# One reciprocal for two row tiles of a softmax, and a list order made anew

## The chip, the cores and the metric

The kernel runs on one core of one Trainium2 chip. The core has a matrix engine (TensorE, PE in the profile), a vector engine (VectorE, DVE), an activation engine (ScalarE, ACT), a general engine (GpSimd, POOL) and a queue that issues most transfers (SyncE, SP). Each engine takes its instructions strictly in the order of the program, and an instruction that waits for another engine holds up all that stand behind it. The metric is the device time of one execution in microseconds (us), the median of several runs.

## The reference

The input is a matrix `x` of 384 rows (nodes of a graph) and 1024 columns, and a list of 6528 edges with a type each. The reference computes a layer norm and a ReLU, three projections, three more projections of their results, a masked softmax attention with 16 heads of width 64, and an output projection with a residual:

```
h = relu(layernorm(x))
q = h @ wq.T + bq;  k = h @ wk.T + bk;  v = h @ wv.T + bv
q2 = heads(q @ wiq.T + biq);  k2 = heads(k @ wik.T + bik);  v2 = heads(v @ wiv.T + biv)
scores = q2 @ k2.T / 8 + mask          # 16 heads, 384 x 384; mask is -inf where there is no edge
attn = softmax(scores)
out = x + concat(attn @ v2) @ wo.T + bo
```

## The kernel before

**Chunks and planes.** Each of the seven weight matrices is cut into eight chunks of 128x1024 (tile `raw`), loaded by SP. The 56 chunks have numbers: 0 to 7 are `wv`, 8 to 15 `wq`, 16 to 23 `wiv`, 24 to 31 `wk`, 32 to 47 are `wiq` and `wik` in turn, 48 to 55 are `wo`. A chunk is split into a high and a low plane (tile `whl`), so that three matmuls of lower precision make up one of high precision: `split_hi` on ACT (L124, L128 in the profile) rounds the chunk, `split_lo` on DVE (L135, L137) takes the rest. The third of a step's three matmuls (L450, L451, L452) needs the low plane. A chunk is eight such steps. `raw` has four buffers, so the load of chunk c waits until the low plane of chunk c-4 is made.

**Sums.** Forty more transfers (tile `scan`, L144) bring weight chunks in once more, and ACT sums their squares or absolute values (L149), for the bounds by which the planes are scaled. They share three buffers.

**The mask.** DVE compares each edge's key with the others, 51 instructions at L295 that are called detections here, to find duplicates; POOL then scatters the edge values to tables in memory (`tab`, L306), which SP had cleared before (L223), and reads them back. The tiles `rows` (L283) hold the keys; they come in three groups of three transfers, for detections 0 to 17, 18 to 35 and 36 to 50. POOL's additions for the mask's diagonal (`mask_base`, L288 and L290) stand among the scatters.

**Attention.** A score tile j = 3p + t is row tile t (128 rows) of head pair p, 24 in all, with two heads o = 0, 1. For each the chain is: `do_S` on PE (L711) into two PSUM banks; `do_ttr` on DVE (L719) adds the mask, writes the tile `e` and the row minimum; `do_exp` on ACT (L723) with the row sum; `recip` and `rscale` on DVE (L726, L730) for both heads of the tile at once; then the normalised values in two planes (tile `pp`): `do_hi` on ACT (L738, L740) and `do_lo` on DVE (L746), or, for a head that a table gives to POOL, `do_norm` on POOL (L733), `do_hi` on ACT and `do_lo` on POOL (L744); then a transposing transfer by SP, and `do_av` on PE (L760). There are four PSUM banks `s` for the scores, so tile j can start when DVE has read tile j-2; six tiles `e`, so the reading of tile j needs the low planes of tile j-3; and three banks `g` for the chunks. `qk_lo` (L702) takes a chunk of `wiq` or `wik` out of its bank; `ao_hi` and `ao_lo` (L764, L767) take the attention's output out. The output projection (`omm`, steps o(a, k) for seven column blocks a and eight chunks k) fills PE between the last score tiles and after them; `finish` (L788) adds the residual and the results leave by transfers of SP and ACT.

**Who sets the order.** The functions above are tasks in a table, each with an engine, an assumed duration and its dependencies. A list scheduler at the end of the kernel repeatedly takes the task that can start first by these assumed times, and among equals the one that is due first. The table `P` at the top holds the numbers that steer it: where score tiles and `do_av` stand in PE's list (`pre`, `rate`, `ds`, `da`), which heads go to POOL (`pool`), the order of the last output steps (`last`), corrections of due times (`due`) and allowances for latency (`slack`, `wait`, `late`, `gate`). On the chip only the order counts; the assumed times are gone.

Of the kernel before, what the change touches and what calls it, by code (L numbers as in the profile page):

```python
# [8 lines left out]
F32 = mybir.dt.float32  # L9
# [15 lines left out]

P = dict(
    pre=11.98,
    rate=2.66,
    avlag=7,
    slack=0.6,  # L30
    act0=6.72,
    dve0=4.77,
    pool0=8.64,
    pb=6,
    lead=3,
    first=[7],
    gate=3.2,
    mll=3.72,
    ds=[0.0, 0.0, 0.0, 0.0, 0.0, 0.0, 0.0, 0.47, 0.47, 0.47, 0.47, 1.09, 0.47, 1.58, 0.47, 0.47, 0.47, 1.04, 0.62,
        0.47, 0.23, 0.47, 0.47, 1.14],  # L40
    da=[1.19, 0.16, 1.23, 1.19, 1.19, -0.39, -0.39, -0.39],
    pool=[0, 1, 0, 1, 0, 1, 0, 1, 0, 1, 0, 1, 0, 1, 0, 1, 0, 1, 0, 1, 0, 1, 0, 1, 0, 0, 0, 1, 0, 1, 0, 1, 0, 1, 0,
        1, 0, 0, 0, 1, 0, 1, 0, 0, 0, 0, 0, 1],
    last=[5, 1, 2, 0, 3, 6, 4],
    sp=dict(row=5.6, bv=41.0, biv=55.0, turn=75.6, kb=88.0, v2t=111.14, gq=118.19, gk=126.86, ob=149.12),
    due=dict(v2l=-0.13, ss=0.11, gkd=-2.65, lo=1.37),
    wait=0.08,
    late=0.27,
    selat=3.85,
    selby=1.62,  # L50
)


# [1 line left out]
def gnn_kernel(ctx: ExitStack, tc: tile.TileContext, x, edges, erows, etw, wq, wk, wv, wiq, wik, wiv, wo,  # L55
# [648 lines left out]
    def do_S(j):  # L704
# [3 lines left out]
        for i, (a, b) in enumerate(((0, 0), (0, 1), (1, 0))):  # L708
            for o in range(2):
                r = slice(o * 64, o * 64 + 64)  # L710
                nc.tensor.matmul(sps[j][o][:, :N], q[r, a, t * 128:(t + 1) * 128], k[r, b, :],  # L711
                                 start=(i == 0), stop=(i == 2))

    def do_ttr(j, o):
        if o == 0:
            sts[j] = work.tile([128, 6], F32, tag="st", name="st", bufs=6)
            es[j] = {}
        es[j][o] = work.tile([128, N], F32, tag="e", name="e", bufs=EB)
        DVE.tensor_tensor_reduce(es[j][o], sps[j][o][:, :N], ma[:, j % 3, :], nscale, 3.0e38, OP.add, OP.min,  # L719
                                 sts[j][:, o:o + 1])  # L720

    def do_exp(j, o):
        ACT.activation(es[j][o], es[j][o], AF.Exp, bias=sts[j][:, o:o + 1], scale=-1.0, accum_out=sts[j][:, 2 + o:3 + o])  # L723

    def recip(j):
        DVE.reciprocal(sts[j][:, 4:6], sts[j][:, 2:4])  # L726

    def rscale(j):

        DVE.tensor_scalar(sts[j][:, 4:6], sts[j][:, 4:6], PSC, None, op0=OP.mult)  # L730

    def do_norm(j, o):
        POOL.tensor_tensor(es[j][o], es[j][o], sts[j][:, 4 + o:5 + o].to_broadcast([128, N]), OP.mult)  # L733

    def do_hi(j, o):
        pls[j, o] = work.tile([128, 2, N], F16, tag="pp", name="pp", bufs=PB)
        if (j, o) in ON_POOL:
            ACT.activation(pls[j, o][:, 0, :], es[j][o], AF.Copy)  # L738
        else:
            ACT.activation(pls[j, o][:, 0, :], es[j][o], AF.Copy, scale=sts[j][:, 4 + o:5 + o])  # L740

    def do_lo(j, o):
        if (j, o) in ON_POOL:
            POOL.tensor_tensor(pls[j, o][:, 1, :], es[j][o], pls[j, o][:, 0, :], OP.subtract)  # L744
        else:
            DVE.scalar_tensor_tensor(pls[j, o][:, 1, :], es[j][o], sts[j][:, 4 + o:5 + o], pls[j, o][:, 0, :],  # L746
                                     op0=OP.mult, op1=OP.subtract)

    def do_turn(j, o):
# [199 lines left out]
    for p in range(8):  # L949
        for n in ("iq", "ik"):  # L950
            c = W0 + 2 * p + (n == "ik")
            chunk_tasks(c)
            for k in range(KT):
                tasks["mm", c, k][3].append(("Qlo" if n == "iq" else "kl", k))
            task(("qhi", c), "ACT", 0.5, lambda c=c: qk_hi(c), [("mm", c, 7)], 0.2, n[1] + "2", [("S", 3 * p + 2)])
            task(("qlo", c), "DVE", 0.53, lambda c=c: qk_lo(c), [("qhi", c)])
        for j in range(3 * p, 3 * p + 3):
            t = j % 3
            task(("S", j), "PE", 0.56, lambda j=j: do_S(j),
                 [("qlo", W0 + 2 * p), ("qlo", W0 + 2 * p + 1), ("S", j - 1)], 0.2, "s s", [("ttr", j, 0), ("ttr", j, 1)])  # L960
            for o in range(2):
                task(("ttr", j, o), "DVE", 0.54, lambda j=j, o=o: do_ttr(j, o),
                     [("S", j), ("ms", j % 3), ("ttr", j, 0) if o else ("ttr", j - 1, 1), ("kf", 7)], 0.2, "e", [("lo", j, o)])
            for o in range(2):
                task(("exp", j, o), "ACT", 0.6, lambda j=j, o=o: do_exp(j, o), [("ttr", j, o)])
            task(("rec", j), "DVE", 0.11, lambda j=j: recip(j), [("exp", j, 0), ("exp", j, 1)])
            task(("rsc", j), "DVE", 0.2, lambda j=j: rscale(j), [("rec", j)])
            for o in range(2):
                pool = (j, o) in ON_POOL
                if pool:  # L970
                    task(("nrm", j, o), "POOL", 0.83, lambda j=j, o=o: do_norm(j, o), [("rsc", j)])
                task(("ehi", j, o), "ACT", 0.41, lambda j=j, o=o: do_hi(j, o),
                     [("nrm", j, o) if pool else ("rsc", j)], 0.2, "pp", [("turn", j, o)])
                task(("lo", j, o), "POOL" if pool else "DVE", 0.87 if pool else 0.55, lambda j=j, o=o: do_lo(j, o), [("ehi", j, o)])
                task(("turn", j, o), "SP", 1.25, lambda j=j, o=o: do_turn(j, o), [("lo", j, o), ("av", p - 2), "pt"], 1.6)
        task(("av", p), "PE", 1.66, lambda p=p: do_av(p),
             [("turn", j, o) for j in range(3 * p, 3 * p + 3) for o in range(2)] + [("av", p - 1)] + [("v2l", i) for i in range(6)],
             0.2, "a", [("aolo", p)])
        task(("aohi", p), "ACT", 0.56, lambda p=p: ao_hi(p), [("av", p), "home"])
        task(("aolo", p), "DVE", 0.53, lambda p=p: ao_lo(p), [("aohi", p)])  # L980
    for i in range(6):
        task(("res", i), "POOL", 1.2, lambda i=i: residual(i), [("xb", i // 2), "bob", ("lo", 23, 1)])
    OFROM = [[("S", J - 1)], [("o", 0, 0)], [("mm", 47, 0)], [("o", 2, 0)], [("o", 1, 0)], [("o", 4, 0)], [("o", 3, 0)]]
# [158 lines left out]
```

## Time and profile before

| what | us |
|---|---|
| median of 3 runs (lowest, highest) | 274.82 (272.44, 275.53) |
| the profiled execution | 274.47 |
| its span, first to last instruction | 272.8 |
| around the span | 1.67 |
| busy in the span: PE, DVE, ACT, POOL | 264.7, 215.4, 207.4, 134.7 |

The profile has a page with shares, slices and groups of instructions, and the trace behind it answers for single stretches. A row of the timeline gives start, duration, engine, line, operation, tiles and shape, and in brackets how long the engine was idle before it and what ended the wait. A matmul's record is longer than the step to the next one, since matmuls are pipelined; the pace is the distance of two starts.

### The profile page before, as it was taken

Reading aid. Unit: us, or ns where it says so; the run is one execution under the profiler, and the core shown is the slowest. Engines: PE = TensorE matmul, PEld = TensorE weight load, DVE = VectorE, ACT = ScalarE, POOL = GpSimd, SP = SyncE. Lnnn points to the kernel's source line nnn. Section 1 sums busy time; section 2 is a strip of 40 time slices with the busy share of each in tenths; the row PEclk is TensorE's granted clock in tenths of the full one; section 3 lists DMA queues with packets and bytes.
Section 4 is the critical chain, followed back from the end, with each engine's and each line's share of the span. In section 5 each row is a group of like instructions: output and inputs, shape, how many; then the busy total and the mean of one; then the engine's idle time right before and its main releaser. Section 6 shows DMA issues by size and latency. Waiting matters only on the chain. (4 is left out here: it accounts for less than half of the span.)

```text
span 272.8 us, 5010 instructions
## 1 busy us (share of the span) xinstructions
PE 264.7 (97%) x1636; PEld 188.3 (69%) x1636; DVE 215.4 (79%) x537; ACT 207.4 (76%) x394; POOL 134.7 (49%) x142
## 2 busy tenths in 40 slices
PE   7899999999999999999999999999999999999994
PEld 6899999999984444899996555555555554444552
DVE  3775578999995675658697999999899899989033
ACT  3886769879897997586978859998989898794100
POOL 5764685545475655466610005556771464335900
PEclk9999999999999999999999999999999999999999
DMA  6899998896999998989899974799999979956415
GB/s 236 267 307 416 369 406 321 221 412 248 353 340 367 382 407 285 320 286 322 268 345 404 356 274 154 118 198 203 231 202 160 248 153 171 324 114 117 87 46 187
DMA packets 58922, 72.44 MB, mean 266 GB/s; under 512 B 42640, under 2 KB 43280, under 8 KB 58896
## 3 DMA queue, kind: packets, MB, share of 16 engines
q1 hardware_dynamic: 56688, 70.26, 83.9%
q0 software_dynamic: 2064, 1.80, 2.3%
q8 instruction: 13, 0.21, 0.3%
q14 instruction: 13, 0.11, 0.1%
q10 hardware_dynamic: 144, 0.07, 0.1%
HBM read 59.27 MB, written 3.39 MB: 230 GB/s over the span
## 5 line engine op out<-in xcount | busy, mean ns | idle before, releaser
L452 PE MATMUL g<-g,whl 128*128 128x384 f32 (+1 forms) x304 | 100.7, 331 | 0.8 <-DVE whl L135 0.5
L450 PE MATMUL g<-g,whl 128*128 128x384 f32 (+1 forms) x304 | 101.3, 333 | 0.0
L451 PE MATMUL g<-g,whl 128*128 128x384 f32 (+1 forms) x304 | 100.6, 331 | 0.0
L306 POOL DMA_INDIRECT tab<-edge x51 | 58.9, 1154 | 40.6 <-DMA tab<-edge 27.2
L149 ACT ACTIVATE scan<-scan 128x1024 f32<-128x1024 f32 x40 | 42.1, 1052 | 16.0 <-DMA scan<-in_wik_dram 5.4
L733 POOL TENSOR_TENSOR e<-e,st 128x384 f32<-128x384 f32 x20 | 22.9, 1146 | 52.7 <-DVE st L726 28.4
L137 DVE TENSOR_TENSOR whl<-raw,whl 128x1024 fp32r<-128x1024 f32 x22 | 27.1, 1230 | 19.2 <-ACT whl L128 12.7
L452 PEld LDWEIGHTS g<-g,whl 128*128 128x128 f32 x176 | 33.0, 188 | 0.6 <-issue 0.6
L450 PEld LDWEIGHTS g<-g,whl 128*128 128x128 f32 x176 | 33.1, 188 | 0.3
L451 PEld LDWEIGHTS g<-g,whl 128*128 128x128 f32 x176 | 33.1, 188 | 0.0
L723 ACT ACTIVATE e<-e,st 128x384 f32<-128x384 f32 x48 | 28.9, 603 | 3.0 <-DVE st L719 3.0
L744 POOL TENSOR_TENSOR pp<-e,pp 128x384 f16<-128x384 f32 x20 | 22.1, 1110 | 15.2 <-ACT pp L738 15.1
L719 DVE CUSTOM_DVE_ANT_0 e<-s,ma,cols 128x384 f32<-128x384 f32 x48 | 27.3, 607 | 0.0
L128 ACT ACTIVATE whl<-raw 128x1024 fp32r<-128x1024 f32 x23 | 24.1, 1048 | 4.1 <-POOL edge L253 2.0
L135 DVE SCALAR_TENSOR_TENSOR whl<-raw,small,whl 128x1024 f16<-128x1024 f32 x16 | 21.0, 1321 | 4.7 <-ACT whl L124 4.7
L450 PE MATMUL s<-whl,g 128*128 128x512 f16 (+2 forms) x65 | 23.6, 363 | 0.5 <-DVE st L719 0.5
L451 PE MATMUL s<-whl,g 128*128 128x512 f16 (+2 forms) x65 | 23.6, 363 | 0.0
L452 PE MATMUL s<-whl,g 128*128 128x512 f16 (+2 forms) x65 | 23.5, 363 | 0.0
L124 ACT ACTIVATE whl<-raw,small 128x1024 f16<-128x1024 f32 x16 | 18.1, 1141 | 5.6 <-DMA raw<-in_wo_dram 4.4
L450 PEld LDWEIGHTS <-whl 128*128 128x128 f16 x128 | 12.5, 98 | 12.1 <-issue 4.9
L135 DVE SCALAR_TENSOR_TENSOR whl<-raw,cols,whl 128x1024 f16<-128x1024 f32 x16 | 20.6, 1294 | 0.0
L746 DVE SCALAR_TENSOR_TENSOR pp<-e,st,pp 128x384 f16<-128x384 f32 x28 | 20.0, 741 | 0.6 <-ACT pp L740 0.5
(184 smaller groups left out, 456.3 us busy)
## 6 DMA issues: line engine op xcount, KB each, us to landing
raw<-in_wv_dram SPq DMA_DIRECT2D x8, 512.0 KB
scan<-in_wiv_dram SPq DMA_DIRECT2D x8, 512.0 KB
raw<-in_wq_dram SPq DMA_DIRECT2D x8, 512.0 KB
scan<-in_wk_dram SPq DMA_DIRECT2D x8, 512.0 KB
raw<-in_wiv_dram SPq DMA_DIRECT2D x8, 512.0 KB
scan<-in_wiq_dram SPq DMA_DIRECT2D x8, 512.0 KB
raw<-in_wk_dram SPq DMA_DIRECT2D x8, 512.0 KB
scan<-in_wik_dram SPq DMA_DIRECT2D x8, 512.0 KB
```

Of the source, the lines that this page charges most:

```text
L128: nc.scalar.activation(hi, raw[w], AF.Copy)
L135: nc.vector.scalar_tensor_tensor(lo, raw[w], sc, hi, op0=OP.mult, op1=OP.subtract)
L137: (eng or nc.vector).tensor_tensor(lo, raw[w], hi.bitcast(F32), OP.subtract)
L149: ACT.activation(x, x, AF.Abs if n in ("iv", "o") else AF.Square, accum_out=l1[:, j, m:m + 1])
L306: nc.gpsimd.indirect_dma_start(out=tabs[c // RNG], out_offset=bass.IndirectOffsetOnAxis(ap=idx[:, c:c + 1], axis=0), in_=val[:, c:c + 1], ...
L450: nc.tensor.matmul(ps, lhi, rhi, start=first, stop=False)
L451: nc.tensor.matmul(ps, lhi, rlo, start=False, stop=False)
L452: nc.tensor.matmul(ps, llo, rhi, start=False, stop=last)
L719: DVE.tensor_tensor_reduce(es[j][o], sps[j][o][:, :N], ma[:, j % 3, :], nscale, 3.0e38, OP.add, OP.min, sts[j][:, o:o + 1])
L723: ACT.activation(es[j][o], es[j][o], AF.Exp, bias=sts[j][:, o:o + 1], scale=-1.0, accum_out=sts[j][:, 2 + o:3 + o])
L733: POOL.tensor_tensor(es[j][o], es[j][o], sts[j][:, 4 + o:5 + o].to_broadcast([128, N]), OP.mult)
L744: POOL.tensor_tensor(pls[j, o][:, 1, :], es[j][o], pls[j, o][:, 0, :], OP.subtract)
```

## The change

Two row tiles now share one tile of statistics (`st`, 12 columns instead of 6): row minima, sums and reciprocals of tiles j and j+1. `recip` and `rscale` run once for an even and an odd tile together, on 128x4 elements instead of twice on 128x2, after the four exponentials of both. So the even tile's normalisation waits for the odd tile's exponentials. There are 12 such pairs of instructions instead of 24.

The scheduler gets one more number, `dl`: it adds to the allowance after a transfer for the tasks that sum (`ss`), so that they stand later in ACT's list, behind tasks that need a weight load. All the steering numbers are new, and the order of every engine is made anew from them: score tiles follow each other more closely in PE's list (`rate`), and the table `pool` gives POOL 19 heads instead of 20.

```diff
-    rate=2.66,
+    rate=2.454,
...
-    late=0.27,
+    late=0.334,
+    dl=0.549,
...
+    def st(j, n, o):
+
+        c = 4 * n + 2 * (j % 2) + o
+        return sts[j // 2][:, c:c + 1]
+
     def do_ttr(j, o):
+        if o == 0 and j % 2 == 0:
+            sts[j // 2] = work.tile([128, 12], F32, tag="st", name="st", bufs=4)
         if o == 0:
-            sts[j] = work.tile([128, 6], F32, tag="st", name="st", bufs=6)
             es[j] = {}
...
     def recip(j):
-        DVE.reciprocal(sts[j][:, 4:6], sts[j][:, 2:4])
+        DVE.reciprocal(sts[j // 2][:, 8:12], sts[j // 2][:, 4:8])
 
     def rscale(j):
 
-        DVE.tensor_scalar(sts[j][:, 4:6], sts[j][:, 4:6], PSC, None, op0=OP.mult)
+        DVE.tensor_scalar(sts[j // 2][:, 8:12], sts[j // 2][:, 8:12], PSC, None, op0=OP.mult)
...
-            task(("rec", j), "DVE", 0.11, lambda j=j: recip(j), [("exp", j, 0), ("exp", j, 1)])
-            task(("rsc", j), "DVE", 0.2, lambda j=j: rscale(j), [("rec", j)])
+            if j % 2:
+                task(("rec", j), "DVE", 0.12, lambda j=j: recip(j), [("exp", i, o) for i in (j - 1, j) for o in range(2)])
+                task(("rsc", j), "DVE", 0.2, lambda j=j: rscale(j), [("rec", j)])
...
+    for j in range(0, J, 2):
+        for o in range(2):
+            tasks[("nrm" if (j, o) in ON_POOL else "ehi", j, o)][3].append(("rsc", j + 1))
...
-                start = max(start, end[d] + (0 if e[0] == eng else e[4] + (P["slack"] if eng == "PE" else P["late"] if e[0] == "SP" else P["wait"])))
+                start = max(start, end[d] + (0 if e[0] == eng else e[4] + (P["slack"] if eng == "PE" else P["late"] + (P["dl"] if n[0] == "ss" else 0.0) if e[0] == "SP" else P["wait"])))
```

Three places show what this does to the order. The line numbers of the changed kernel are one higher in its first part and seven higher from `do_ttr` on.

**DVE, detections and the low planes of chunks 6 and 7.** L295 is a detection, L137 the low plane of a chunk, L479 takes a `wv` chunk out of its bank, L301 and L302 make scatter indices. Before, from the low plane of chunk 6 (first row) to those of chunks 7 and 8 (last row but one, `x2`):

```order
L137 TENSOR_TENSOR whl<-raw,whl 128x1024
L295 SCALAR_TENSOR_TENSOR junk,edge<-rows,edge,upper 128x128
L301 SCALAR_TENSOR_TENSOR ed<-edge 128x3x2
L302 TENSOR_SCALAR edge<-ed,small 128x3x2
L295 SCALAR_TENSOR_TENSOR junk,edge<-rows,edge,upper 128x128 x4
L479 TENSOR_TENSOR f<-g,rrow 128x384 x2
L137 TENSOR_TENSOR whl<-raw,whl 128x1024 x2
L295 SCALAR_TENSOR_TENSOR junk,edge<-rows,edge,upper 128x128 x2
```

In the changed kernel the same place, from six detections ahead of the low plane of chunk 6 to the low plane of chunk 7 (L138, last row):

```order
L296 SCALAR_TENSOR_TENSOR junk,edge<-rows,edge,upper 128x128 x6
L138 TENSOR_TENSOR whl<-raw,whl 128x1024
L480 TENSOR_TENSOR f<-g,rrow 128x384
L302 SCALAR_TENSOR_TENSOR ed<-edge 128x3x2
L303 TENSOR_SCALAR edge<-ed,small 128x3x2
L296 SCALAR_TENSOR_TENSOR junk,edge<-rows,edge,upper 128x128 x9
L302 SCALAR_TENSOR_TENSOR ed<-edge 128x3x3
L303 TENSOR_SCALAR edge<-ed,small 128x3x3
L138 TENSOR_TENSOR whl<-raw,whl 128x1024
```

Ahead of the low plane of chunk 7, eleven detections and two index pairs that stood behind it now stand ahead, and one L479 went behind it. On SP the third clear of a table now stands ahead of the load of chunk 5 instead of behind it, one transfer of `rows` ahead of the load of chunk 6, and the last three transfers of `rows` around the loads of chunks 9 and 10, several transfers earlier than before. On POOL `mask_base` stands behind the sixth scatter instead of the third.

**DVE, the reciprocals of tiles 8 and 9.** Tile numbers stand in the names (`st_2287` is tile 8's, `st_2302` tile 9's). Before:

```order
L726 RECIPROCAL st_2287<-st_2287 128x2
L730 TENSOR_SCALAR st_2287<-st_2287 128x2
L702 SCALAR_TENSOR_TENSOR q2_2316<-g_2198,cols_277,q2_2316 128x384
L726 RECIPROCAL st_2302<-st_2302 128x2
L730 TENSOR_SCALAR st_2302<-st_2302 128x2
L767 SCALAR_TENSOR_TENSOR g1_1732<-a_2228,small_97,g1_1732 128x384
```

Changed, from the second head of tile 9 (L726 is now `do_ttr`, L136 a low plane of weights, L753 a low plane of the softmax):

```order
L726 ISA e_2319,st_2250<-s_2260,ma_105,cols_277 128x384
L726 ISA st_2250 128x1
L136 SCALAR_TENSOR_TENSOR whl_2059<-raw_2005,cols_277,whl_2059 128x1024
L753 SCALAR_TENSOR_TENSOR pp_2297<-e_2191,st_2158,pp_2297 128x384
L733 RECIPROCAL st_2250<-st_2250 128x4
L737 TENSOR_SCALAR st_2250<-st_2250 128x4
```

One pair of instructions on four columns has taken the place of two pairs.

**ACT, between the exponentials of tiles 5 and 6.** L723 (L730 after the change) is an exponential, L740 and L738 (L747 and L745) are high planes of the softmax, L124 (L125) is the high plane of a weight chunk, L696 (L697) that of a `q2` or `k2` tile. Before, from the last exponential of tile 5:

```order
L723 ACTIVATE e_2111,st_2083<-e_2111,st_2083 128x384
L740 ACTIVATE pp_2147<-e_2067,st_2066 128x384
L738 ACTIVATE pp_2150<-e_2076 128x384
L740 ACTIVATE pp_2172<-e_2084,st_2083 128x384
L723 ACTIVATE e_2168,st_2167<-e_2168,st_2167 128x384
L723 ACTIVATE e_2177,st_2167<-e_2177,st_2167 128x384
```

Changed:

```order
L730 ACTIVATE e_2119,st_2056<-e_2119,st_2056 128x384
L125 ACTIVATE whl_2146<-raw_2054,cols_277 128x1024
L125 ACTIVATE whl_2161<-raw_2097,cols_277 128x1024
L747 ACTIVATE pp_2174<-e_2057,st_2056 128x384
L745 ACTIVATE pp_2179<-e_2066 128x384
L730 ACTIVATE e_2159,st_2158<-e_2159,st_2158 128x384
L730 ACTIVATE e_2168,st_2158<-e_2168,st_2158 128x384
```

Two weight planes now stand between the exponentials of tile 5 and the high planes of tile 4.

On PE the number of matmuls is the same. The work that went behind a score tile is: for tile 10 five chunk steps, for tiles 8 and 11 four, for tile 20 one chunk step and eight output steps, for tile 23 six output steps. Seven score tiles that ran in pairs back to back now stand in two places (7 pairs and 10 single tiles instead of 11 and 2). The last `do_av` has three output steps more ahead of it, and the last output block is one of 256 columns instead of one of 512.

More of the change, by code (lines that the diff above doesn't have):

```diff
@@ L27 @@
     pre=11.98,
-    rate=2.66,
+    rate=2.454,
     avlag=7,
[L30 to L33, printed above, removed]
+    slack=0.619,
+    act0=6.919,
+    dve0=5.054,
+    pool0=8.306,
     pb=6,
@@ L36 @@
     first=[7],
[L37 to L42, printed above, removed]
+    gate=3.474,
+    mll=3.761,
+    ds=[0.0, -0.08, 0.0, 0.0, 0.0, 0.0, 0.0, 0.02, 0.47, 0.47, -0.35, 0.27, -0.35, 1.49, 0.38, 0.38, 0.38, -0.86,
+        0.53, 0.38, 0.14, 0.38, 0.37, 1.04],
+    da=[1.19, 0.16, 0.44, 0.69, -1.09, -1.16, -1.16, -1.72],
+    pool=[0, 1, 0, 1, 0, 1, 0, 1, 0, 1, 0, 1, 0, 1, 0, 1, 0, 1, 0, 1, 0, 1, 0, 1, 0, 0, 0, 1, 0, 0, 0, 1, 0, 0, 1,
         1, 0, 0, 0, 1, 0, 1, 0, 0, 0, 0, 0, 1],
-    last=[5, 1, 2, 0, 3, 6, 4],
-    sp=dict(row=5.6, bv=41.0, biv=55.0, turn=75.6, kb=88.0, v2t=111.14, gq=118.19, gk=126.86, ob=149.12),
-    due=dict(v2l=-0.13, ss=0.11, gkd=-2.65, lo=1.37),
+    last=[1, 0, 2, 6, 3, 4, 5],
+    sp=dict(row=5.6, bv=41.0, biv=55.55, turn=75.6, kb=88.0, v2t=111.14, gq=118.19, gk=126.86, ob=147.73),
+    due=dict(v2l=5.14, ss=0.11, gkd=-1.36, lo=1.37),
     wait=0.08,
-    late=0.27,
-    selat=3.85,
-    selby=1.62,
+    late=0.334,
+    dl=0.549,
+    selat=4.065,
+    selby=1.991,
 )
@@ L719, in do_ttr @@
         DVE.tensor_tensor_reduce(es[j][o], sps[j][o][:, :N], ma[:, j % 3, :], nscale, 3.0e38, OP.add, OP.min,
-                                 sts[j][:, o:o + 1])
+                                 st(j, 0, o))
     def do_exp(j, o):
-        ACT.activation(es[j][o], es[j][o], AF.Exp, bias=sts[j][:, o:o + 1], scale=-1.0, accum_out=sts[j][:, 2 + o:3 + o])
+        ACT.activation(es[j][o], es[j][o], AF.Exp, bias=st(j, 0, o), scale=-1.0, accum_out=st(j, 1, o))
     def recip(j):
-        DVE.reciprocal(sts[j][:, 4:6], sts[j][:, 2:4])
+        DVE.reciprocal(sts[j // 2][:, 8:12], sts[j // 2][:, 4:8])
     def rscale(j):
-        DVE.tensor_scalar(sts[j][:, 4:6], sts[j][:, 4:6], PSC, None, op0=OP.mult)
+        DVE.tensor_scalar(sts[j // 2][:, 8:12], sts[j // 2][:, 8:12], PSC, None, op0=OP.mult)
     def do_norm(j, o):
-        POOL.tensor_tensor(es[j][o], es[j][o], sts[j][:, 4 + o:5 + o].to_broadcast([128, N]), OP.mult)
+        POOL.tensor_tensor(es[j][o], es[j][o], st(j, 2, o).to_broadcast([128, N]), OP.mult)
     def do_hi(j, o):
@@ L739, in do_hi @@
         else:
-            ACT.activation(pls[j, o][:, 0, :], es[j][o], AF.Copy, scale=sts[j][:, 4 + o:5 + o])
+            ACT.activation(pls[j, o][:, 0, :], es[j][o], AF.Copy, scale=st(j, 2, o))
     def do_lo(j, o):
@@ L745, in do_lo @@
         else:
-            DVE.scalar_tensor_tensor(pls[j, o][:, 1, :], es[j][o], sts[j][:, 4 + o:5 + o], pls[j, o][:, 0, :],
+            DVE.scalar_tensor_tensor(pls[j, o][:, 1, :], es[j][o], st(j, 2, o), pls[j, o][:, 0, :],
                                      op0=OP.mult, op1=OP.subtract)
```

## The prediction

> **What bounds the kernel now.** I read the page first, its busy shares and its slices.
>
> ```profile
> span 272.8 us, 5010 instructions
> ...
> PE 264.7 (97%) x1636; PEld 188.3 (69%) x1636; DVE 215.4 (79%) x537; ACT 207.4 (76%) x394; POOL 134.7 (49%) x142
> ...
> PE   7899999999999999999999999999999999999994
> ...
> PEclk9999999999999999999999999999999999999999
> ```
>
> PE is busy in 97% of the span, in every slice but the first two and the last at 90% or more, at full clock. The number of matmuls stays. So time can only come from gaps in PE's row, and from what stands after its last matmul. The second view is stretches of the attention stage (columns: sum of the stretch, then busy time of PE, PE's weight loads, DVE, ACT, POOL, then granted clock, DMA share, GB/s).
>
> ```profile
> 160.00:200.00 40.00, 40.00 (x286) 21.98 (x285) 37.88 (x102) 38.14 (x86) 21.96 (x21) 1.00 0.85 182
> 226.00:247.00 21.00, 19.98 (x139) 9.96 (x136) 19.80 (x50) 17.67 (x41) 8.03 (x6) 1.00 0.90 201
> ```
>
> From 160 to 200 us PE never waits, though DVE and ACT are 95% busy behind it. From 226 to 247 PE loses 1.0 us and DVE is 94% busy. DVE's time is near the bound there and nowhere else counts. The third view is PE's timeline, searched for starts that are further apart than the step.
>
> ```profile
> 41.57 0.34 PE L451 MATMUL g<-g,whl 128*128 128x384 f32 x1
> 42.23 0.45 PE L452 MATMUL g<-g,whl 128*128 128x384 f32 x1 [0.32 <-issue]
> ...
> 148.97 0.33 PE L451 MATMUL g<-g,whl 128*128 128x384 f16 x1
> 149.80 0.34 PE L452 MATMUL g<-g,whl 128*128 128x384 f16 x1 [0.51 <-DVE whl L135]
> ...
> 232.58 0.38 PE L452 MATMUL g<-whl,g 128*128 128x512 f16 x1
> 233.51 0.27 PE L450 MATMUL g<-whl,g 128*128 128x256 f16 x1 [0.56 <-DVE k L702]
> ...
> 245.84 0.38 PE L452 MATMUL s<-whl,g 128*128 128x512 f16 x1
> 246.68 0.27 PE L450 MATMUL s<-whl,g 128*128 128x256 f16 x1 [0.46 <-DVE st L719]
> ```
>
> Four stalls carry nearly all. Start to start they are 0.66, 0.83, 0.93 and 0.84; less the usual step (0.17 for 384 columns, 0.21 to 0.22 for 512) they lose **0.49, 0.66, 0.72 and 0.62**, together 2.5 us. The first waits for the low plane of chunk 7, the second for that of chunk 33, the third for a bank that `qk_lo` of chunk 47 must empty, the fourth for the bank of the second head of tile 23. These four are all that a better order can win; the paired reciprocal can touch only the last two.
>
> **The change, part by part.** The sum is made against the profiled execution's 274.47 us, which is 0.35 below the median of 274.82, so the two stand for each other.
>
> *The reciprocals themselves.*
>
> ```profile
> 239.71 0.17 DVE L726 RECIPROCAL st<-st 128x2 f32<-128x2 f32 x1 [0.67 <-ACT e L723]
> 239.90 0.17 DVE L730 TENSOR_SCALAR st<-st 128x2 f32<-128x2 f32 x1
> 239.98 1.28 DVE L135 SCALAR_TENSOR_TENSOR whl<-raw,small,whl 128x1024 f16<-128x1024 f32 x1
> ...
> 15.13 0.17 DVE L342 RECIPROCAL lnt<-lnt 128x3 f32<-128x3 f32 x1
> ```
>
> From the reciprocal's start to the start of what follows the scaling is 0.27. No row has a reciprocal on four columns; three cost the same 0.17 as two, so four are taken at 0.17, and at most 0.34. Twelve pairs go: 12 x 0.27 = 3.2 us of DVE (1.2 if four columns cost twice). By the windows this hides behind PE except near the end.
>
> *(A) Chunk 7.*
>
> ```profile
> 32.12 0.34 DVE L295 SCALAR_TENSOR_TENSOR junk<-rows,edge,upper 128x128 bf16<-128x128 f32 x1
> 35.51 0.35 DVE L301 SCALAR_TENSOR_TENSOR ed<-edge 128x6 f32<-128x6 f32 x1
> 36.04 0.59 DVE L295 SCALAR_TENSOR_TENSOR junk<-rows,edge,upper 128x128 bf16<-128x128 f32 x1
> 36.57 0.60 DVE L295 SCALAR_TENSOR_TENSOR junk<-rows,edge,upper 128x128 bf16<-128x128 f32 x1
> 38.12 1.01 DVE L479 TENSOR_TENSOR f<-g,rrow 128x384 f32<-128x384 f32 x2
> 40.94 1.23 DVE L137 TENSOR_TENSOR whl<-raw,whl 128x1024 fp32r<-128x1024 f32 x1 [1.82 <-ACT f L483]
> ...
> 36.55 0.46 POOL L290 TENSOR_TENSOR ma<-ma,d 128x128 f32<-128x128 f32 x1
> ...
> 32.89 1.06 ACT L128 ACTIVATE whl<-raw 128x1024 fp32r<-128x1024 f32 x1
> ```
>
> Before, DVE idled 1.82 ahead of this low plane, which ended at 42.17. Now the high plane of chunk 6 (32.89) comes some 1.2 later, since a `rows` transfer goes ahead of its load: it ends at 35.15, its low plane at about 36.5. Then come one L479 (0.5), two index pairs (0.53 each, 35.51 to 36.04), nine detections and the low plane (1.23). A detection takes 0.34 alone and 0.60 beside POOL's `mask_base`: the pitch there is 0.53 (36.04 to 36.57), alone 0.26 less, 0.27. All alone the chain ends at 36.5 + 0.5 + 1.06 + 9 x 0.27 + 1.23 = 41.7; with five of them beside `mask_base`, which now stands three scatters later, at 43.1. Against 42.17 that is -0.49 (no stall at all is the floor) to +0.95. I take a middle, **+0.3**, because POOL's later place falls beside the last detections rather than the first.
>
> The same two rows bear on a rule. The Trainium skill, page "SBUF — State Buffer", section "Who interferes with whom", says that a VectorE instruction with two inputs in SBUF contends with a GpSimd instruction that reads SBUF, and that the second one blocks. By that rule all detections beside `mask_base` pay, and A would be +0.9 instead of +0.3, the sum 0.6 higher. The trace agrees as far as it goes (0.34 alone, 0.60 beside).
>
> *(B) Chunk 33.* The stall of 0.66 follows late weights; the sums (L149) now stand behind the weight planes in ACT's list, which should free ACT for them, but the loads themselves keep their slots on SP. If the sum had been the cause, all 0.66 goes; if a load comes one place later, 0.3 is added. I take **-0.1**, nearest to "nothing moved".
>
> *(C) The last two stalls.*
>
> ```profile
> L746 DVE SCALAR_TENSOR_TENSOR pp<-e,st,pp 128x384 f16<-128x384 f32 x28 | 20.0, 741 | 0.6 <-ACT pp L740 0.5
> ...
> L135 DVE SCALAR_TENSOR_TENSOR whl<-raw,cols,whl 128x1024 f16<-128x1024 f32 x11 | 14.3, 1303 | 0.0
> ...
> L719 DVE CUSTOM_DVE_ANT_0 e<-s,ma,cols 128x384 f32<-128x384 f32 x48 | 27.3, 607 | 0.0
> ```
>
> Ahead of `qk_lo` of chunk 47, DVE's list loses ten reciprocal pairs (2.7), the low planes of chunks 50 and 51 (2.6) and one L746 (0.74), and gains two L746 (1.48) and the two L719 of tile 20 (1.21): 3.35 us less, while the step that needs the bank stands only 0.7 earlier. Ahead of the L719 of tile 23 it has 2.6 us less by the same count, and the step that needs that bank stands 1.9 later. Each margin is over its stall, so both vanish: **-1.34**; 0 if ACT, 17.67 of 21 busy there, holds DVE up for as much.
>
> *(D) The new wait.* An even tile's normalising now waits for the odd tile's exponentials, and ACT must do two weight planes between those and the high planes. DVE's instruction behind them waits, and behind it stand the L719 that free the score banks.
>
> ```profile
> 186.61 1.15 ACT L124 ACTIVATE whl<-raw,cols 128x1024 f16<-128x1024 f32 x1
> ...
> 189.78 0.60 DVE L719 CUSTOM_DVE_ANT_0 e<-s,ma,cols 128x384 f32<-128x384 f32 x1
> ...
> 193.40 1.15 PE L711 MATMUL s<-k,q 64*128 64x384 f16 x12
> ```
>
> Tile 9's banks are read by 190.38 (189.78 + 0.60), tile 11 needs them at 193.40: 3.0 us of slack before. Tile 11 now stands four chunk steps (8 x 3 matmuls of 0.165 are a whole chunk; four steps are 2.0) earlier; ahead of tile 9's L719 four pairs went (1.1) and about as much came. So some 1.1 to 1.3 is left, and the two planes can hold ACT for 2.2. Between no stall and one such tile at its full 2.2 - 1.1 = 1.1, with some more behind, I take **+0.3** of 0 to 1.5, nearest to the window 160 to 200, in which PE never waited.
>
> *(E) Score pairs split.*
>
> ```profile
> 164.74 0.66 PE L711 MATMUL s<-k,q 64*128 64x384 f16 x6
> 165.33 0.34 PE L450 MATMUL g<-g,whl 128*128 128x384 f16 x1
> ...
> 234.26 1.15 PE L711 MATMUL s<-k,q 64*128 64x384 f16 x12
> 235.34 0.28 PE L450 MATMUL g<-whl,g 128*128 128x256 f16 x1
> ```
>
> A pair of score tiles takes 1.08 of PE, a single one 0.59: 0.10 more for each of the four pairs split, **+0.4**; 0 if singles elsewhere cost no more than half a pair.
>
> *(F) The tail.*
>
> ```profile
> 269.08 0.88 DVE L788 SCALAR_TENSOR_TENSOR g<-s,small,g 128x384 f32<-128x384 f32 x2 [0.82 <-PE s L452]
> ```
>
> The last output block has 256 columns instead of 512, but a block of 512 finishes nearer to the end, ahead of it on DVE: **+0.2** (0 to +0.4, half of this row).
>
> Sum: 0.3 - 0.1 - 1.34 + 0.3 + 0.4 + 0.2 = -0.24, so 274.47 - 0.2 = **274.3 us**.
>
> **The rivals.** *Slower: the pair's latency.*
>
> ```profile
> L733 POOL TENSOR_TENSOR e<-e,st 128x384 f32<-128x384 f32 x20 | 22.9, 1146 | 52.7 <-DVE st L726 28.4 <-DVE st L730 22.2 <-ACT e L723 1.3
> ...
> L744 POOL TENSOR_TENSOR pp<-e,pp 128x384 f16<-128x384 f32 x20 | 22.1, 1110 | 15.2 <-ACT pp L738 15.1
> ```
>
> POOL waited 50 us for reciprocals before, so each is used at once: the chain of normalise, high plane, low plane (1.15 + 0.5 + 1.11) starts later by as much as the odd tile is behind the even one, and six `e` tiles hold only three score tiles. From the point where DVE's wait for the high planes passes the 1.2 left in D, each odd tile stalls PE. With 0.8 to 1.0 for tiles 9, 11 and 13 (2.2 less 1.2 to 1.4), 2.4 to 3.0, and C not won because DVE arrives late as well: 274.47 + 0.3 - 0.1 + 0.4 + 0.2 + 2.7 = **278.0**. For it: DVE and ACT at 95%. Against it: PE had no gap from 160 to 200, and DVE gets 3.2 us. Chance 0.24.
>
> *Faster: all goes.* A at its floor, B's 0.66 gone, C's 1.34 gone, no new wait: 274.47 - 2.49 + 0.1 for splits = **272.1**. For it: each has a cause of its own that the order touches. Chance 0.18.
>
> *The change does nothing to the time.* DVE's 3.2 us are eaten by waits for ACT, C is 0, and A and B cancel: 274.47 + 0.4 + 0.2 - 0.4 = **274.7**. For it: ACT's 38.14 of 40 are not reduced. Chance 0.16.
>
> **How the numbers follow.** My forecast has the rest, 0.42. The range runs from 271.6, just below the faster case with B or the splits a little better, to 278.5, the slower case with 0.5 more on a tile; that leaves out under 2 in 10. The likeliest case alone has 273.0 to 275.7. A measurement of this kernel can tell about 1%, 2.7 us, from no change. The faster case passes that line about as often as not, and a little comes from luck in A and B together: 0.17 faster. The slower case passes it nearly always, and a late load early on adds some: 0.26 slower. The rest, 0.57, is the same.
>
> **What would show it.** A: the low plane of chunk 7 ends between 41.7 and 43.1, with detections of 0.6 beside `mask_base`. B: a gap of about 0.6 near 149 stays. C: no waits for L702 and L719 near 232 and 246. D: idle time on DVE ahead of L753 by ACT's L747, and a gap of at most 1 us ahead of tile 11. The reciprocal's row: 12 of 128x4 at about 0.16. E: PE's total for L711 some 0.4 higher by starts. F: PE's last matmul to the end as before, 3.7, within 0.4. The forecast is wrong if PE's gaps between 170 and 215 exceed 1.5 us, or if chunk 7 or a load before it is late by over 1.

## The result, and the profile after

The median fell from 274.39 (272.44 to 276.74) to **272.19** (271.6 to 275.79), 20 executions each. The ratio of the two is 0.9939 with an interval of 0.9915 to 0.9963: 0.6% faster, clear of no change, and less than the 1% that the prediction set as its line. Forecast were 274.3, within a range of 271.6 to 278.5. The median is nearer to the rival "faster: all goes" (272.1) than to the likeliest case.

The profiled execution took 274.23, 0.24 less than that of before and 2 us more than the median of its own kernel; 13 of the 20 executions lie between 271.6 and 272.25, the others from 273.2 on. So its rows hold waits that most executions can't have. Its page:

```profile
span 272.2 us, 4983 instructions
...
PE 265.5 (98%) x1636; PEld 188.0 (69%) x1636; DVE 212.0 (78%) x514; ACT 207.6 (76%) x394; POOL 127.6 (47%) x140
```

PE is as busy as before. DVE lost 3.4 us and 23 instructions, POOL 7 us. The same two stretches, with the columns as before:

```profile
160.00:200.00 40.00, 39.37 (x275) 20.75 (x275) 35.72 (x89) 36.00 (x83) 17.71 (x20) 1.00 0.88 177
226.00:247.00 21.00, 21.00 (x144) 10.61 (x139) 19.91 (x40) 15.91 (x35) 6.25 (x5) 1.00 1.09 195
```

The late stretch is now full (21.00 of 21.00, before 19.98), with DVE as busy as before. The stretch from 160 to 200, in which PE never waited, now has waits. PE's timeline at the places of interest:

```profile
41.59 0.34 PE L452 MATMUL g<-g,whl 128*128 128x384 f32 x1
42.02 0.44 PE L453 MATMUL g<-g,whl 128*128 128x384 f32 x1
...
177.55 1.60 PE L712 MATMUL s<-k,q 64*128 64x384 f16 x12
...
193.45 0.35 PE L767 MATMUL a<-pt,vhl 128*64 128x384 f16 x1
194.20 1.62 PE L767 MATMUL a<-pt,vhl 128*64 128x384 f16 x17 [0.40 <-DMA pt<-pp]
```

The wait for chunk 7 is 0.43 less the step of 0.17, 0.26. Those near 149, 232 and 246 are gone. A pair of score tiles (L712 x12) takes 1.60 where one without a wait has 1.15, and a `do_av` waits for a transposing transfer in two pieces: 0.85 in all, counted from the step ahead of it.

Counted the same way over the whole row, PE's last matmul ends 0.60 earlier (268.44 against 269.04):

| part | forecast | profiled execution | profiles of two near copies (below) |
|---|---|---|---|
| A, chunk 7 | +0.3 | -0.23 | -0.48 |
| B, chunk 33 | -0.1 | -0.67 | -0.67 |
| C, the two late stalls | -1.34 | -1.34 | -1.34 |
| D, new waits | +0.3 | +0.7 at score tiles, +0.85 at a `do_av` | -0.2 |
| E, pairs split | +0.4 | +0.7 | +0.7 |
| F, tail | +0.2 | 0.0 | 0.0 |
| small waits near 133, 153 and 242, not in the forecast | 0 | -0.5 | -0.5 |

The rows of the profiled execution add up to -0.5, steps too small to name bring PE's row to -0.60, and 0.36 more around the span leaves -0.24. That this agrees with the forecast of -0.2 is luck: the misses cancel there. In the two near copies D's waits are missing, which fits the lower median. One caution holds for the whole table: its base is one execution of the kernel before, and a second one, below, has neither B's wait nor the small ones. So these two rows, 1.2 us together, are not shown to belong to the change.

### The profile page after: what moved, and what is told of

The parts are those of the page before. It is cut to its first block, busy times and chain, and to the rows that moved or that the text cites. A ratio compares the mean times of both kernels' runs of the same rounds, so it can differ in the third digit from the quotient of the medians.

```text
span 272.2 us, 4983 instructions
## 1 busy us (share of the span) xinstructions
PE 265.5 (98%) x1636; PEld 188.0 (69%) x1636; DVE 212.0 (78%) x514; ACT 207.6 (76%) x394; POOL 127.6 (47%) x140
## 4 chain that ended last, share of the span: by engine, by line
PE 76%; DMA 8%; DVE 7%; ACT 3%; issue 3%; POOL 2%; SPq 0%; DVEq 0%; POOLq 0%; ACTq 0%
PE g L451 17%; PE g L453 16%; PE g L452 16%; PE s L451 5%; PE s L453 5%; PE s L452 5%; PE a L767 4%; DMA raw<-in_wik_dram 4%; PE s L712 2%; DMA g<-in_x_dram 2%; DMA pt<-pp 2%; PE g L833 2%; PE g L688 2%; ACT e L730 2%; DVE e L726 1%
## 5 line engine op out<-in xcount | busy, mean ns | idle before, releaser
L307 POOL DMA_INDIRECT tab<-edge x51 | 60.8, 1192 | 41.2 <-DMA tab<-edge 23.3
L740 POOL TENSOR_TENSOR e<-e,st 128x384 f32<-128x384 f32 x19 | 17.6, 940 | 51.0 <-DVE st L737 48.1
L138 DVE TENSOR_TENSOR whl<-raw,whl 128x1024 fp32r<-128x1024 f32 x22 | 27.0, 1226 | 14.7 <-ACT whl L129 7.2
L730 ACT ACTIVATE e<-e,st 128x384 f32<-128x384 f32 x48 | 28.9, 604 | 2.0 <-DVE st L726 1.6
L751 POOL TENSOR_TENSOR pp<-e,pp 128x384 f16<-128x384 f32 x19 | 17.9, 942 | 26.3 <-ACT pp L745 26.2
L726 DVE CUSTOM_DVE_ANT_0 e<-s,ma,cols 128x384 f32<-128x384 f32 x48 | 28.2, 612 | 2.3 <-PE s L712 0.8
L136 DVE SCALAR_TENSOR_TENSOR whl<-raw,small,whl 128x1024 f16<-128x1024 f32 x16 | 20.8, 1326 | 6.4 <-ACT whl L125 6.4
L125 ACT ACTIVATE whl<-raw,cols 128x1024 f16<-128x1024 f32 x16 | 17.9, 1141 | 7.6 <-DMA raw<-in_wik_dram 4.2
L136 DVE SCALAR_TENSOR_TENSOR whl<-raw,cols,whl 128x1024 f16<-128x1024 f32 x16 | 22.5, 1414 | 1.4 <-ACT whl L125 1.4
L125 ACT ACTIVATE whl<-raw,small 128x1024 f16<-128x1024 f32 x16 | 18.0, 1141 | 5.3 <-DMA raw<-in_wo_dram 3.8
```

The lines of the kernel that those rows point to most:

```text
L125: nc.scalar.activation(hi, raw[w], AF.Copy, scale=sc)
L136: nc.vector.scalar_tensor_tensor(lo, raw[w], sc, hi, op0=OP.mult, op1=OP.subtract)
L138: (eng or nc.vector).tensor_tensor(lo, raw[w], hi.bitcast(F32), OP.subtract)
L307: nc.gpsimd.indirect_dma_start(out=tabs[c // RNG], out_offset=bass.IndirectOffsetOnAxis(ap=idx[:, c:c + 1], axis=0), in_=val[:, c:c + 1], ...
L730: ACT.activation(es[j][o], es[j][o], AF.Exp, bias=st(j, 0, o), scale=-1.0, accum_out=st(j, 1, o))
```

## Experiments: which waits are always there

The first three are the two kernels once more and a copy without the new number. First the changed kernel, unaltered.

> The changed kernel a second time, with nothing altered. Its profiled execution took 274.23, its median 272.19, so that profile shows about 2 us that most executions don't have. Theory 1: they are waits inside PE's row (1.7 us of waits between 164 and 194, the largest 0.85 ahead of the do_av at 193, for a transposing transfer). Then a profile near 272 has its last matmul near 266.5, with these waits gone. Theory 2: they lie behind the last matmul, in the output's transfers. Then a profile near 272 has its last matmul at 268.4 again and ends 1.7 instead of 3.75 later. Median 272.2 by both.

Measured: median 272.58 (271.67 to 275.61), ratio 0.9972 (0.9927 to 1.0017). Its profiled execution took 273.26, with the last matmul at 267.51 and the end 3.73 behind it. The wait at `do_av` is gone, the first score tiles wait 0.26, and the pair near 177.5 still waits 0.36. The wait near 149 is there (0.60), with another cause; DVE's timeline:

```profile
146.00 1.52 DVE L319 COPY_PREDICATED ma<-mbs 128x1152 f32<-128x1152 int32 x1 [1.56 <-DMA mbs<-tab]
147.41 1.28 DVE L136 SCALAR_TENSOR_TENSOR whl<-raw,cols,whl 128x1024 f16<-128x1024 f32 x1
```

The low plane of chunk 33 stands behind the copy of the mask, which waited 1.56 for the read-back of the scattered tables. Theory 1 holds in kind, though this execution is not near 272: what differs between the two is in PE's row. The tail was 3.72 before, 3.75 and 3.73 in the two profiles of the changed kernel.

The kernel before, unaltered:

> The kernel before a second time, with nothing altered, for which of its waits come back in another execution. Theory 1: the two late ones (0.72 near 232, 0.62 near 246) belong to the order and return within 0.2; the one near 149 (0.67) hangs on when a load lands and may be anything from 0 to 2. Theory 2: all four are fixed by the order and return within 0.2.

Measured: median 274.92 (272.48 to 276.87), ratio 1.0042 (0.9998 to 1.0086). The program is the same, so 0.4% between two runs is no difference yet. In its profile (273.33) the two late stalls return, at 0.75 and 0.61, chunk 7 waits 0.80, and the wait near 149 is not there. Theory 1 holds: C's stalls belong to the order of the lists, and B's wait comes and goes from one execution to the next.

The allowance for sums at zero:

```diff
-    dl=0.549,
+    dl=0.0,
```

> The changed kernel with the allowance for sums (dl) at 0: PE's and POOL's lists stay, ACT's, DVE's and SP's differ only before about 150 us. Theory 1, the later sums keep the weight planes from waiting: a wait of 0.6 to 0.8 near 149 is there in each execution, median 0.5 to 0.8 above the changed kernel. Theory 2, what decides near 149 is when the loads land: the median stays within 0.3, and the wait may be there or not.

Measured: median 272.10 (271.45 to 274.19), ratio 0.9966 (0.9930 to 1.0002), as the changed kernel. In its profile (271.59) PE has no wait near 42, 149, 177 or 193, and its last matmul ends at 265.83. Theory 2: the new number, the one part of the change that names the sums, is worth nothing here. This profile is of a fast execution, 0.5 below the median.

What did change near 149 is where the sums wait. ACT's groups from 100 to 156 us, of the kernel before and of the changed one:

```profile
L149 ACT ACTIVATE scan<-scan 128x1024 f32<-128x1024 f32 x19 | 20.0, 1054 | 11.7 <-DMA scan<-in_wik_dram 5.4 <-DMA scan<-in_wo_dram 5.1 <-DMA scan<-in_wiq_dram 1.0
```

```profile
L150 ACT ACTIVATE scan<-scan 128x1024 f32<-128x1024 f32 x19 | 19.9, 1048 | 3.7 <-DMA scan<-in_wik_dram 2.1 <-DMA scan<-in_wo_dram 1.7
```

ACT waited 11.7 us at its sums for their loads, now 3.7 (6.5 in the changed kernel's second profile, 4.8 with `dl` at zero). But the kernel before waited 9.9 in its second profile, and 5.4 with paired reciprocals and all numbers of before (a run below), so what moved them is not shown. The four planes from chunk 33 on started at 146.63 before (146.04 and 145.17 in those two), and now here:

```profile
144.20 4.27 ACT L125 ACTIVATE whl<-raw,cols 128x1024 f16<-128x1024 f32 x4 [1.60 <-issue]
```

## Experiments: is it DVE's time?

In the changed kernel each paired instruction is taken apart where it stands, and nothing is moved:

```diff
-        DVE.reciprocal(sts[j // 2][:, 8:12], sts[j // 2][:, 4:8])
+        for c in (8, 10):
+            DVE.reciprocal(sts[j // 2][:, c:c + 2], sts[j // 2][:, c - 4:c - 2])
...
-        DVE.tensor_scalar(sts[j // 2][:, 8:12], sts[j // 2][:, 8:12], PSC, None, op0=OP.mult)
+        for c in (8, 10):
+            DVE.tensor_scalar(sts[j // 2][:, c:c + 2], sts[j // 2][:, c:c + 2], PSC, None, op0=OP.mult)
```

> The changed kernel with the paired reciprocal taken apart and nothing moved: at each of the 12 places two reciprocals on 128x2 and two scalings on 128x2 in place of one and one on 128x4, 24 instructions more on DVE, some 2.5 to 3.2 us. Theory 1, the gain is from where things stand in the lists: the median stays within 0.4 of the changed kernel's (272.2 to 272.6). Theory 2, the two late stalls went because DVE had 2.7 us less ahead of qk_lo of chunk 47: about 1 to 1.3 comes back (273.2 to 273.5), and as waits of PE for L703 and L726 between 226 and 247.

Measured: median 273.32 (271.66 to 276.33), 6 executions, ratio 0.9978 (0.9929 to 1.0027): too wide to tell. But its profile has no wait for L703 or L726 from 226 to 247. So it ran again:

> Once more the changed kernel with each paired reciprocal and scaling taken apart in its place, for its time: the first had few executions and a wide spread (271.7 to 276.3). Theory 1, DVE's time is worth nothing by itself: within 0.5 of the changed kernel's 272.2 and a clean row of PE from 226 to 247. Theory 2: it costs 1 or more.

Measured: median **272.57** (271.95 to 274.28), ratio 0.9943 (0.9908 to 0.9978), beside the changed kernel's 0.9939. The row of PE from 226 to 247 has one wait, at a `do_av` for its transposing transfer (0.39), none for DVE. Theory 1: the 24 instructions saved are worth some 0.4 us by the medians; the intervals leave room for about 1. The prediction's own margins allow that: ahead of `qk_lo` of chunk 47 they were 3.35 - 0.7 - 0.72 = 1.9. The test is also smaller than it was meant to be: taken apart, reciprocals and scalings cost 6.3 us of DVE in the first profile and 5.6 in the second, against 4.7 in the changed kernel's, which is 0.9 to 1.6 more and not 2.5 to 3.2.

Then the single reciprocals with all new numbers, each with its own tile's exponentials and a tile of statistics for each, as before, so that the scheduler lists everything anew:

```diff
-            if j % 2:
-                task(("rec", j), "DVE", 0.12, lambda j=j: recip(j), [("exp", i, o) for i in (j - 1, j) for o in range(2)])
-                task(("rsc", j), "DVE", 0.2, lambda j=j: rscale(j), [("rec", j)])
+            task(("rec", j), "DVE", 0.11, lambda j=j: recip(j), [("exp", j, 0), ("exp", j, 1)])
+            task(("rsc", j), "DVE", 0.2, lambda j=j: rscale(j), [("rec", j)])
```

> All new numbers and the allowance for sums, but the reciprocals as before: one on 128x2 for each of the 24 tiles, right behind its own exponentials, listed anew by the scheduler. Theory 1, the places make the gain: within 0.4 of the changed kernel (272.2 to 273.0), no waits between 226 and 247, and less waiting for the score tiles near 165 and 177 (0.4 there in the changed kernel), since no tile waits for its odd neighbour. Theory 2, the paired reciprocal is needed for it: at least 1 of waits between 226 and 247, 273.5 or more.

Measured: median **278.26** (277.05 to 279.9), ratio 1.0193 (1.0138 to 1.0247): theory 2, and much more than it asked for. PE's row has waits for DVE at score tiles and at output steps, the largest of them these:

```profile
192.24 0.64 PE L712 MATMUL s<-k,q 64*128 64x384 f16 x5 [1.01 <-DVE st L720]
...
238.53 0.38 PE L451 MATMUL s<-whl,g 128*128 128x512 f16 x1 [0.87 <-DVE st L720]
...
255.69 0.39 PE L453 MATMUL g<-whl,g 128*128 128x512 f16 x1 [0.93 <-DVE g L768]
```

This kernel and the taken-apart one both have 24 reciprocals on 128x2 and the same numbers; they are 2.5% apart. So what counts is the order of the lists, not the number of instructions. A row that differs is the reciprocal's, from 155 to 250 us, here of this kernel and then of the changed one:

```profile
L727 DVE RECIPROCAL st<-st 128x2 f32<-128x2 f32 x24 | 3.7, 157 | 2.9 <-ACT e L724 2.9
```

```profile
L733 DVE RECIPROCAL st<-st 128x4 f32<-128x4 f32 x12 | 2.0, 171 | 1.0 <-ACT e L730 1.0
```

DVE waited 2.9 us at the reciprocals for the exponentials ahead of them. With reciprocals at every second tile it is 1.0 here, 0.3 in the changed kernel's second profile, 0.4 and 0.0 in the two profiles of the taken-apart kernel, and 2.5 and 1.9 before. That such waits on an engine 90% busy are what the pair removes fits these rows; the lists differ in more than this, and no run isolated it. Nor were new numbers sought for single reciprocals in any run, so a good order without the pair is not ruled out. The reciprocal's duration on four columns, 0.17, was taken rightly; the scaling took 260 ns on average before, more than the 0.17 of the row that was forecast from.

## Experiments: the parts of the order

Paired reciprocals with all numbers of before:

```diff
     late=0.27,
+    dl=0.0,
```

> Paired reciprocals alone, with all the numbers of before. Theory 1, the pair saves DVE 3.2 us but that is worth nothing by itself: early waits as before (about 1.2), and the late ones are as large as with the new early part and the old attention (1.5 near 229, 1.5 near 237) or larger: 274.5 to 276. Theory 2, the relief of DVE alone removes the two late waits (-1.34): 273.0.

Measured: median 273.67 (271.71 to 276.84), ratio 1.0008 (0.9964 to 1.0051): no change. In its profile the two late stalls are gone, a new one of 0.38 stands at the last pair of score tiles, and chunk 7 waits 0.80. Neither theory had this: relief did take the late stalls, as theory 2 has it, and the time didn't follow. Part of it is behind PE's last matmul: from there to the end of the execution are 5.98 here, 5.43 and 5.49 in the two profiles of before.

New early numbers with single reciprocals and the attention's numbers (`rate`, `ds`, `da`, `pool`, `last`) of before:

> The kernel before with single reciprocals and the attention's numbers of before (rate, ds, da, pool, last), and all other numbers new, so that the lists up to about 150 are those of the changed kernel. Theory 1, the early part is worth what its waits were (0.5 to 0.9 near 42, 0 to 0.8 near 149): the median is 0.8 to 1.4 below the kernel before, and the late waits of 0.72 and 0.62 are still there. Theory 2, what comes early is lost again later, since DVE is 95% busy in the attention either way: within 0.4 of the kernel before.

Measured: median 276.42 (275.13 to 278.95), ratio 1.0104 (1.0064 to 1.0145). **Slower than before**, though PE has no wait at chunk 7 or chunk 33. The gain is lost in the attention, where PE waits for DVE:

```profile
192.76 0.64 PE L712 MATMUL s<-k,q 64*128 64x384 f16 x5 [0.74 <-DVE st L720]
...
235.34 1.72 PE L761 MATMUL a<-pt,vhl 128*64 128x384 f16 x18 [1.14 <-DVE g L768]
...
238.82 0.64 PE L712 MATMUL s<-k,q 64*128 64x384 f16 x5 [1.00 <-DVE st L720]
```

Both theories took the late part of the list for given. It is not: the scheduler lists the attention anew from where the early part ends, and DVE then waited 3.5 us at the reciprocals.

Paired reciprocals, the attention's numbers new and all others of before:

> Paired reciprocals and the new numbers for the attention's order (rate, ds, da, pool, last); all other numbers, and so every list up to about 150 us, as before. Theory 1, early waits count one for one: those before 150 (0.48 near 41, 0.22 near 133, 0.79 near 149 and 153) come back in place of 0.26: 272.2 + 1.2 = 273.4. Theory 2, the attention alone makes the gain, and what is late early on is caught up: 272.2.

Measured: median 275.93 (273.2 to 277.51), 6 executions, ratio 1.0045 (0.9995 to 1.0095), so nothing is gained without the early part, and perhaps something lost. Theory 2 falls, and theory 1's 273.4 is missed by more than 2; its profile is of the slowest of the six executions, and no row of it is used here. The reverse, early numbers new, the attention's of before:

> Paired reciprocals, with the attention's order from the numbers of before (rate, ds, da, pool, last) and all other numbers new. Theory 1: the early waits are gone (-1.2) and the two late ones too, because DVE has 2.7 us less (-1.3): 274.4 - 2.5 = 271.9. Theory 2, the late gain was the new places of score tiles and output steps: the late waits stay, 274.4 - 1.2 = 273.2, and waits for the odd tile's exponentials may add to it.

Measured: median 273.83 (272.96 to 276.04), ratio 1.0014 (0.9970 to 1.0059). The early waits are gone and the late ones larger than before, 1.50 near 229 and 0.98 near 237:

```profile
230.46 0.27 PE L451 MATMUL g<-whl,g 128*128 128x256 f16 x1 [1.34 <-DVE k L703]
```

Theory 2: with early numbers and pairs alone nothing is won. Two more runs take the attention's numbers apart. First the order of the last output blocks:

```diff
-    last=[1, 0, 2, 6, 3, 4, 5],
+    last=[5, 1, 2, 0, 3, 6, 4],
```

> The changed kernel with the order of the last output blocks of before (last). Lists differ only from about 238 us. Theory 1, the late wait for tile 23's bank went because the steps that need that bank stand later: it comes back, 0.5 to 1, near 240, median 272.7 to 273.2. Theory 2, DVE's shorter list is enough: no wait, 272.2, and the tail behind the last matmul within 0.4 of 3.7.

Measured: median 272.16 (271.45 to 274.06), ratio 0.9954 (0.9920 to 0.9988), no wait from 226 to 247, last matmul at 265.81, tail 3.75. Theory 2: the later step that needs tile 23's bank was not needed for C, and the last blocks are worth nothing either way.

Then the places of score tiles and `do_av` (`rate`, `ds` and `da` of before, all else new):

> The changed kernel with the places of score tiles and do_av of before (rate, ds, da), with the new heads for POOL and the new last blocks. Theory 1, these places are what the paired reciprocal needs, because it makes banks and e tiles late: waits of 1 to 3 at score tiles or at chunk 47, median 273.2 to 275. Theory 2, heads for POOL and last blocks made the gain: within 0.4 of 272.2, and 0.7 less of PE for score tiles, whose pairs are whole again.

Measured: median 274.0 (273.25 to 275.33), ratio 0.9996 (0.9959 to 1.0033). All of the gain is gone. PE waits 0.96 at a score tile, 1.35 behind a `do_av` for chunk 47's bank and 0.43 behind the last pair, for tile 23's bank:

```profile
193.09 0.64 PE L712 MATMUL s<-k,q 64*128 64x384 f16 x5 [0.64 <-DVE st L726]
...
232.67 0.27 PE L451 MATMUL g<-whl,g 128*128 128x256 f16 x1 [1.28 <-DVE k L703]
```

That is 2.7 of waits; score tiles in whole pairs save 0.7; so 2.0 should be lost, and the median is 1.8 above the changed kernel's. Theory 1: these places carry C and keep D small.

## Why the prediction came out as it did

**The bound was read rightly, the sum was not.** PE's row decided. The range held the time because it took in the rival in which all goes, to which 0.18 was given; the likeliest case, 273.0 to 275.7, did not. In the two copies at 271.6 the last matmul ends 3.2 us earlier than in before's profile: 3.0 of waits named in the prediction or in the table went, 0.2 ahead of the first score tiles too, the splits took 0.7, and the other 0.7 is spread over steps too small to name, most of it ahead of 30 us.

**A failed in one step:** five detections were put beside POOL's `mask_base`. DVE's and POOL's timelines:

```profile
39.97 0.35 DVE L296 SCALAR_TENSOR_TENSOR junk<-rows,edge,upper 128x128 bf16<-128x128 f32 x1
...
40.76 1.21 DVE L138 TENSOR_TENSOR whl<-raw,whl 128x1024 fp32r<-128x1024 f32 x1
...
43.96 0.48 DVE L296 SCALAR_TENSOR_TENSOR junk<-rows,edge,upper 128x128 bf16<-128x128 f32 x1
...
37.87 1.10 POOL L307 DMA_INDIRECT tab<-edge  x1 [3.44 <-DVE ed L302]
...
41.61 0.61 POOL L289 TENSOR_TENSOR d<-ident,small 128x128 f32<-128x128 f32 x1
```

`mask_base` began at 41.61, when all nine detections were done at 0.35 each. The chain ended at 41.97; "all alone" was worked out at 41.7. (It began later than forecast, since the low plane of chunk 6 ended at 37.07 and not at 36.5, but the two index pairs took 0.7 and not 1.06.) In the changed kernel's second profile it ended at 40.87, and PE had no stall. POOL's three scatters ahead of it were taken to follow at once, but the first of them waited 3.44 for its indices. So the Trainium skill's rule on VectorE and GpSimd ("SBUF — State Buffer", "Who interferes with whom") did not come into play at this place. The next detection, at 43.96, stands beside POOL's work and takes 0.48.

**B's price is open.** "Nothing moved" looked at SP's slots alone. The weight planes did come earlier, by 2.4 us in the two profiles compared (146.63 to 144.20). But the stall of 0.66 had been taken for a fixed cost of the old order, and it was not: PE has no wait at chunk 33 in the second profile of the kernel before, nor with pairs alone and all numbers of before. In the new order it has none either, but for the 0.60 behind the copy of the mask. What the new order is worth at this place is not shown.

**C was right in size and place, and its reason only in part.** A shorter list of DVE ahead of the two places fits both stalls' going. Of what was counted, the ten reciprocal pairs were not needed (the kernel taken apart), nor the later step (the old last blocks). The places of the score tiles and `do_av` were, with the new early lists; with pairs alone, on the places of before, both stalls went too. The low planes of chunks 50 and 51 were not tried apart.

**D had a mechanism that was there, at the wrong tile.** DVE did wait longer ahead of its low planes for ACT's high planes (1.7 in all, 0.5 before), but nothing waits at tile 11. Of the 3.5 us from the last read of tile 9's banks to the start of tile 11, 0.24 are left, and 0.66 with `dl` at zero. (The forecast had 3.0 and 1.1 to 1.3; 193.40 is the start of tile 10, the first of that pair.) The largest wait at score tiles is at the pair of tiles 6 and 7; DVE:

```profile
176.76 0.62 DVE L726 CUSTOM_DVE_ANT_0 e<-s,ma,cols 128x384 f32<-128x384 f32 x1 [0.81 <-POOL pp L751]
...
177.31 0.61 DVE L703 SCALAR_TENSOR_TENSOR k<-g,cols,k 128x384 f16<-128x384 f32 x1
```

DVE waits 0.81 for POOL's low plane to free a tile `e`, and behind it stands the low plane of the `k2` tile that ends at 177.92; the pair that began at 177.55 goes on at 177.97. This is the slower rival in small: six `e` tiles and a chain that starts later. The rival asked for three tiles with 0.8 to 1.0; the profiled execution had 0.5 at this pair and 0.4 together at two other places, the second one 0.36 here, and the copies at 271.6 had none. So its price never came. The 2.7 with the places of before are not shown to be it, since single reciprocals with all numbers new wait for DVE still more.

**E was forecast too small:**

```profile
190.20 0.33 PE L453 MATMUL g<-g,whl 128*128 128x384 f16 x1
190.46 0.66 PE L712 MATMUL s<-k,q 64*128 64x384 f16 x6
191.05 0.34 PE L451 MATMUL g<-g,whl 128*128 128x384 f16 x1
```

The forecast counted from the score tile's start (0.59). From the step ahead, 190.20, to the step behind is 0.85, less one step of 0.165: 0.69 against 1.18 for a pair, so a split costs 0.20, not 0.10. Four splits, with one tile more beside a `do_av`, make 0.7. **F** was nothing: 3.72 before, 3.75 after.

## What to carry to other kernels

Where one engine is full and its helpers are at 90%, count the order as one thing: here the early lists, the score tiles' places and the paired reciprocal gave -0.6% together, and 0 to +1.9% in every run that lacked one of the three. Each of those runs is one list, made anew by the scheduler, and not the best one without that part. The instructions saved were worth little by themselves; that DVE asks for the exponentials at 12 places instead of 24 came with the gain. And a wait in one profile is a draw from many: run the same kernel again before putting a price on it.

## What had not been expected

POOL's normalising (L733, then L740) took 1146 ns on average before and 940 after, its low planes 1110 and 942, and DVE's low planes (L746, then L753) 741 and 678, with the same shapes:

```profile
L740 POOL TENSOR_TENSOR e<-e,st 128x384 f32<-128x384 f32 x19 | 17.6, 940 | 51.0 <-DVE st L737 48.1 <-DMA pt<-pp 2.8
...
L753 DVE SCALAR_TENSOR_TENSOR pp<-e,st,pp 128x384 f16<-128x384 f32 x26 | 17.3, 678 | 1.7 <-ACT pp L747 1.7
```

What decides is the instruction that stands behind the scaling in DVE's list. Here are, in the kernel before, a low plane of weights that DVE began right behind a scaling, and the normalising on POOL that the scaling had released:

```profile
198.87 1.28 DVE L135 SCALAR_TENSOR_TENSOR whl<-raw,cols,whl 128x1024 f16<-128x1024 f32 x1
...
199.11 1.73 POOL L733 TENSOR_TENSOR e<-e,st 128x384 f32<-128x384 f32 x1 [1.08 <-DVE st L730]
```

Row by row, POOL's normalising takes 0.82 to 0.83 us, except where a low plane had begun on DVE some 0.2 us ahead of it: 1.06 to 1.14 behind one of the softmax, 1.73 to 1.79 behind one of weights. Before, that was so for 4 and 6 of the 20, and after for 1 and 2 of the 19. The mean was 933 with pairs alone, 966 with single reciprocals and all numbers new, and 1169 with the new early numbers and single ones, so neither the pair nor the numbers set it alone. How much of the time this is was not measured apart.

The time around the span rose from 1.67 to 2.03. Counted from PE's last matmul to the end of the execution it is 5.43 and 5.49 in the two profiles of before, 5.75 to 5.79 in those of the changed kernel and of the two near copies, and 5.88 to 5.98 in those of the pairs taken apart, of pairs alone and of the old places. It takes 0.3 us of the gain in PE's row; its cause is open.
